# A channel-by-channel FFT convolution stage: the column part of a shift read from memory instead of multiplied by a matrix

## The chip, the cores and the metric

One core of one Trainium2 chip runs the whole program in one launch. The metric is device time in microseconds (us) of that core; the time of a kernel is the median of several executions. A profile is one more execution, recorded by the hardware: instructions of TensorE (PE; its weight loads are PEld), VectorE (DVE), ScalarE (ACT), GpSimd (POOL), the DMA issues of SyncE (SP), and the packets of 16 DMA engines.

## The reference

Four layers with residuals on x of 32 images x 192 channels x 56 x 56, float32. Each layer normalizes its input over 32 groups of 6 channels.

```python
x = x + _L0_conv_ref(_gn(x), ...)   # agent attention, depthwise 3x3 convolution, projection
x = x + _L1_conv_ref(_gn(x), ...)   # bidirectional recurrent scan over the 3136 positions
x = x + _L2_conv_ref(_gn(x), L2_conv_offset)
x = x + _L3_conv_ref(_gn(x), ...)   # 55x55 depthwise convolution with a computed filter, plus bias * x
```

The change is about layer 2. 48 offsets of two numbers each serve four channels apiece. An offset is rounded to a whole shift R in y and x, with zeros where the source lies outside the image; what is left of it, delta, sets a 3x3 Gaussian kernel, which is the product of three row factors and three column factors:

```python
out = shift_one(x, R)                       # zeros from outside
sq = (f[None, None, :] + delta[:, 0]) ** 2 + (f[None, :, None] + delta[:, 1]) ** 2
kern = exp(-sq / (2 * 0.5 ** 2)); kern = kern / kern.sum(axis=(1, 2))
out_LO = conv3x3_depthwise(out, kern, padding=1)
```

Since a layer works on a normalized input, (x - m) / sqrt(var + eps), the kernel keeps the mean m and the factor 1/sqrt(var + eps) beside x and applies them where they fit.

## The kernel before

The program has four stages one after the other: `make_filter` computes the filter of layer 3 and its spectra; `attention` does layer 0 image by image; `scan_pairs` does layer 1 on pairs of images; `channel_blocks` does layers 2 and 3 channel by channel. The first two overlap at their seam and end at about 5180 us, the scan runs to 8360, the channel stage from there to the end. `scan_guarded` is a slower scan that is entered only for extreme values.

**x2.** The scan hands its result to the channel stage through x2 in device memory, laid out as [channel][image parity s][row h, 57 of them][16 image pairs g][56 columns]. The 57th row holds the mean that the normalization needs. One channel is 114 partitions (s, h) x 896 (g, w) floats; a partition's 896 floats lie together, 3584 bytes. rs2 holds the factor 1/sqrt(var + eps) of each channel and image.

**Steps of the channel stage.** The 192 channels form 32 groups of 6, the groups of layer 3's normalization. The loop at the end of `channel_blocks` runs n over 33 values and j over 6; one (n, j) is called a step here. In a step, channel j of group n-1 is analysed (`analyse`), channel j-1 is finished (`synthesise`, the generator `ending`), and group n is prepared: two channels are shifted in each step with j below 3 (`shift`), two are centred in each with j of 3 to 5 (`centre`). The parts are generators, and a written-out order takes turns between them, so that TensorE has matmuls of one part while another waits for its evictions. A scheduler keeps each engine's order close to this; instructions of an engine run in order.

**Shift before.** For one channel `shift` loads x (L1582, on SP's queue), and multiplies from both sides by matrices: eight matmuls (L1589) with the row matrix, which also moves rows and subtracts the mean, then eight (L1607) with the column matrix. VectorE evicts the first with the factor 1/sqrt (L1596), adds the second product to x (L1615, two instructions of 114x448) and sums rows for the next normalization (L1616). The two matrices are made once in four channels by GpSimd (`matrices`, L1542, L1546, L1547), and the row matrix passes once through TensorE (L1550, L1552).

**Centre, analyse, synthesise.** `centre` subtracts the group's mean on VectorE (L1633), squares on ScalarE (L1635) and sums on VectorE (L1636); L1641 and L1642 make layer 3's factor rs from the means (L1624). `analyse` turns rows to spectra with eight matmuls (L1757 in `_rows_to_spectra`; ScalarE copies them out at L1763), columns with six (L1655), and multiplies by the filter's spectrum on VectorE (L1662 to L1668, eighteen instructions). `synthesise` goes back with 32 matmuls (L1681), whose results ScalarE copies out as four z pieces of 84x448 (L1688), and four more (L1698); VectorE multiplies the result by rs (L1700) and adds it to x (L1701), and SP stores x in two halves (L1704).

**Buffers.** x has 15 buffers, the ring `ps` in PSUM four, most work tiles two. x's buffer comes free with the store.

**Start.** The shifts, the Gaussian factors and the validity masks are computed at the beginning of `channel_blocks` by some thirty small operations on 114 partitions.

**SP's queue.** All the loads and stores named here are issued by SyncE, in order. In `attention` it loads the next image while one is worked on, and stores x1 at an image's end. In a step of the channel stage it issues two output stores, the load of a channel and, once a group, factors and spectra.

Of the kernel before, what the change touches and what calls it, by code (L numbers as in the profile page):

```python
# [20 lines left out]
F32 = mybir.dt.float32  # L21
# [7 lines left out]
C = 192  # L29
T = 96  # L30
# [37 lines left out]

def _resize_matrix():

    at = (np.arange(S) + 0.5) * POOL / S - 0.5
    w = np.maximum(0.0, 1.0 - np.abs(at[:, None] - np.arange(POOL)[None, :]))
    return w / w.sum(1, keepdims=True)
# [4 lines left out]
    (114, (2 * 2 * NF,)), (128, (2, 2 * NF)), (84, (2, 2 * S)), (84, (2, 114)), (114, (114,)), (114, (114,)),  # L78
    (114, (114,)), (112, (112,)), (114, (2,)),
# [3 lines left out]
def _constants():  # L83
# [16 lines left out]
    for t in range(2):  # L100
# [17 lines left out]
        "chan_k": _filled([f[n] for n in "f1 f2 f3 f4 ones_rows lags diff_y diff_x at_rows".split()]),  # L118
# [3 lines left out]
def _spectral_constants():  # L122
# [21 lines left out]
    for s in range(2):  # L144
# [7 lines left out]
    col = np.arange(2 * S) % S  # L152
    together = np.arange(2 * S)[:, None] // S == np.arange(2 * S)[None, :] // S
    diff_x = np.where(together, col[None, :] - col[:, None], 1e6)
    at_rows = np.stack([np.concatenate([col, [0, 0]]), row], 1)
# [5 lines left out]
        "ones_rows": ones,  # L161
        "lags": lags,
        "diff_y": diff_y,
        "diff_x": diff_x,
        "at_rows": at_rows,
# [41 lines left out]

@with_exitstack
def make_filter(ctx: ExitStack, tc: tile.TileContext, a, consts, filt, spectra, beside):
# [29 lines left out]
    beside()  # L239
    nd = cp.tile([T, 2], F32, name="nd", tag="nd")  # L240
# [124 lines left out]
def attention(ctx: ExitStack, tc: tile.TileContext, a, ready, x1, st_a, st_c):  # L365
# [48 lines left out]
    for t in (*agents_b[0], *agents_b[1], v_a, v_c):  # L414
        nc.gpsimd.memset(t, 0.0)

# [342 lines left out]
    for b in range(NB):  # L759
# [57 lines left out]
        for h, r in HALVES:  # L817
            nc.sync.dma_start(out=x1[b, 128:C, 1568 * h : 1568 * h + 1568], in_=x[1][r].rearrange("p y x -> p (y x)"))
# [32 lines left out]
def scan_pairs(ctx: ExitStack, tc: tile.TileContext, a, k, x1, st_a, st_c, x2, rs2, count):  # L851
# [86 lines left out]
    kept_a, kept_c = small("kept_a", [128, 2, NB // 4, 2]), small("kept_c", [128, 2, NB // 4])  # L938
# [261 lines left out]
    def conclude(s):  # L1200
# [3 lines left out]
        nc.vector.tensor_copy(kept_a[:, p % 2, p // 2, :], rs[:, 0:2, 0])  # L1204
        nc.vector.tensor_copy(kept_c[:, p % 2, p // 2 : p // 2 + 1], rs[:, 2])
# [46 lines left out]
    for i, r in enumerate((slice(0, 64), slice(64, 128))):  # L1252
        nc.sync.dma_start(out=rs2[128:C, :, :, i], in_=kept_c[r])
# [17 lines left out]
def scan_guarded(ctx: ExitStack, tc: tile.TileContext, a, k, x1, x2, rs2):  # L1271
# [45 lines left out]
    kept = cp.tile([T, 2, 2, NB // 4, 2], F32, name="kept", tag="kept")  # L1317
# [47 lines left out]
    for b in range(NB):  # L1365
# [84 lines left out]
        g, i = b // 4, b // 2 % 2  # L1450
        nc.vector.tensor_copy(kept[:, :, i, g, b % 2], rs)
# [11 lines left out]
def channel_blocks(ctx: ExitStack, tc: tile.TileContext, a, k, x2, rs2, spectra, out):  # L1463
# [11 lines left out]
    PR = 2 * (S + 1)  # L1475
# [6 lines left out]

    NP = C // 4
    off = cp.tile([PR, NP, 2], F32, name="off", tag="off")
    nc.sync.dma_start(out=off, in_=a["L2_conv_offset"].partition_broadcast(PR))
# [8 lines left out]
    f1, f2, f3, f4, ones, lags, diff_y, diff_x, at = pieces  # L1494
# [6 lines left out]
    nc.vector.tensor_scalar(off, off, -(2.0**21), 2.0**21, ALU.max, ALU.min)  # L1501
    rnd = cp.tile([PR, NP, 2], F32, name="rnd", tag="rnd")
    nc.vector.tensor_scalar(rnd, off, BIG, None, ALU.add)
    nc.vector.tensor_scalar(rnd, rnd, BIG, None, ALU.subtract)
    gs = cp.tile([PR, NP * 2, 3], F32, name="gs", tag="gs")
    nc.vector.tensor_tensor(off, off, rnd, ALU.subtract)
    flat = off.rearrange("p n d -> p (n d)")
    for f in range(3):
        nc.vector.tensor_scalar(gs[:, :, f], flat, float(f - 1), None, ALU.add)
    nc.vector.tensor_tensor(gs, gs, gs, ALU.mult)  # L1510
    nc.scalar.activation(gs, gs, AF.Exp, scale=-2.0)
# [384 lines left out]
```

## Time and profile before

| | us |
|---|---|
| median of 3 runs | 12302.43 (12298.38 to 12305.09) |
| profiled execution, time | 12294.66 |
| profiled execution, span | 12292.8 |

Busy time in us by stage, from windows of the trace:

| stage | length | PE | DVE | ACT | POOL | granted PE clock | DMA share |
|---|---|---|---|---|---|---|---|
| filter and attention, 110 to 5180 | 5070 | 4793.9 | 4349.8 | 2771.6 | 177.4 | 0.97 | 0.16 |
| scan, 5180 to 8360 | 3180 | 2644.7 | 3063.2 | 2026.6 | 1753.0 | 0.93 | 0.41 |
| start of channel stage, 8360 to 8420 | 60 | 24.9 | 30.1 | 2.3 | 34.8 | 0.73 | 0.36 |
| channel stage, 8420 to 12150 | 3730 | 3681.9 | 3235.0 | 1330.5 | 283.4 | 1.00 | 0.17 |
| its last steps, 12150 to 12293 | 143 | 134.9 | 104.9 | 52.0 | 0.0 | 0.99 | 0.14 |

The DMA share is the mean busy share of all 16 engines: a transfer that runs on six of them alone shows at most 0.38. A float32 matmul leaves two records, and records of successive matmuls and VectorE operations overlap a little, so a mean duration is longer than the distance from one instruction to the next.

### The profile page before, as it was taken

The numbers are of one execution on the slowest core, as the hardware profiler recorded it, in microseconds if no ns is written. First come the engines' busy times: TensorE is split into PE (matmuls) and PEld (weight loads), VectorE is DVE, ScalarE is ACT, GpSimd is POOL, SyncE is SP. The second block draws the span as 40 slices with busy tenths as digits, with TensorE's granted clock in tenths as the row PEclk, the third lists the DMA queues.
The fourth block names the chain that finished last, engine by engine and source line by source line (L and its number), as shares of the span: only waits on it lengthen the run. The fifth ranks groups of instructions, "written<-read, shape, count | busy, mean of one in ns | idle before, by whom it ended". The sixth has DMA issues, their size and how long they took to land. (4 is left out here: it accounts for less than half of the span.)

```text
span 12292.8 us, 164375 instructions
## 1 busy us (share of the span) xinstructions
PE 11329.2 (92%) x62734; PEld 7107.7 (58%) x62734; DVE 10836.4 (88%) x15489; ACT 6205.0 (50%) x11808; POOL 2250.7 (18%) x2228
## 2 busy tenths in 40 slices
PE   7999999999999999788888888888999999999999
PEld 3555555655555555333333333336777777777777
DVE  6888888888888887999999999997888888888888
ACT  3555555555555554566666666663333333333333
POOL 0000000000000000655555555551000000000000
PEclk9999999999999999999999999999999999999999
DMA  2111111111111111244344433442111111111111
GB/s 69 40 42 46 52 41 40 40 40 40 40 40 40 42 50 44 75 103 100 95 97 103 101 94 97 103 101 65 44 41 45 41 44 42 44 42 44 42 43 29
DMA packets 930055, 719.69 MB, mean 59 GB/s; under 512 B 770325, under 2 KB 807236, under 8 KB 920124
## 3 DMA queue, kind: packets, MB, share of 16 engines
q1 hardware_dynamic: 919020, 683.39, 21.7%
q10 hardware_dynamic: 10240, 25.70, 0.8%
q8 instruction: 500, 8.19, 0.3%
q14 instruction: 295, 2.42, 0.1%
HBM read 403.47 MB, written 240.65 MB: 52 GB/s over the span
## 5 line engine op out<-in xcount | busy, mean ns | idle before, releaser
L572 DVE SCALAR_TENSOR_TENSOR o<-v_a,att_w,o 128x896 f32<-128x896 f32 (+1 forms) x1024 | 1053.8, 1029 | 418.6 <-ACT v_a L546 291.5
L1763 ACT COPY y<-ps 64x252 f32<-64x252 f32 (+1 forms) x2376 | 808.2, 340 | 1135.0 <-PE ps L1757 1104.8
L1681 PE MATMUL ps<-fixed,real 84*84 84x112 f32 x6144 | 1090.9, 259 | 0.0
L1681 PE MATMUL ps<-fixed,imag 84*84 84x112 f32 x6144 | 1089.5, 259 | 0.0
L1688 ACT COPY z<-ps 84x448 f32<-84x448 f32 x768 | 405.6, 528 | 1218.5 <-PE ps L1681 1217.0
L1086 POOL MEMSET f<- 128x1 f32 x96 | 8.9, 99 | 4726.3 <-DMA st_c<-st 4721.3
L1681 PEld LDWEIGHTS ps<-fixed,real 84*84 84x84 f32 x6144 | 784.0, 153 | 134.2 <-issue 95.8
L1681 PEld LDWEIGHTS ps<-fixed,imag 84*84 84x84 f32 x6144 | 763.8, 153 | 0.0
L1079 ACT ACTIVATE q<-q 128x784 f32<-128x784 f32 x384 | 328.2, 855 | 802.5 <-DVE q L1074 633.1
L834 PE MATMUL ps<-sq,fixed 128*128 128x392 f32 x512 | 297.3, 743 | 428.6 <-ACT sq L1157 428.6
L572 DVE SCALAR_TENSOR_TENSOR o<-v_c,att_w,o 128x448 f32<-128x448 f32 (+1 forms) x1024 | 635.0, 620 | 5.1
L585 PE MATMUL ps<-xs_a,gk_a 128*98 128x448 f32 (+1 forms) x1536 | 637.1, 495 | 0.0
L589 ACT ACTIVATE pr<-ps,low 98x896 f32<-98x896 f32 (+1 forms) x384 | 352.3, 918 | 559.9 <-DVE low L587 559.9
L586 PE MATMUL ps<-xs_c,gk_c 125*98 125x448 f32 (+1 forms) x1536 | 631.6, 492 | 0.0
L1547 POOL TENSOR_TENSOR mat<-tap,tap 114x114 f32<-114x114 f32 x96 | 40.8, 425 | 3166.1 <-PE ps L1607 2313.2
L677 PE MATMUL ps<-gq_a,xs_a 128*112 128x294 f32 x1792 | 602.8, 417 | 19.2 <-DVE pq L682 19.2
L1698 PE MATMUL ps<-z,fixed 84*114 84x448 f32 x1536 | 608.8, 539 | 0.0
L834 PE MATMUL ps<-x,weights 128*128 128x392 f32 x1536 | 577.4, 519 | 27.5 <-DVE bv L1108 14.2
L678 PE MATMUL ps<-gq_c,xs_c 125*112 125x294 f32 x1792 | 594.5, 412 | 0.0
L1655 PE MATMUL re<-y,fixed 128*84 128x420 f32 (+1 forms) x1152 | 532.3, 543 | 8.7 <-ACT y L1763 7.6
L1655 PE MATMUL im<-y,fixed 128*84 128x420 f32 (+1 forms) x1152 | 526.9, 538 | 0.0
L690 ACT ACTIVATE pq<-pq 112x1176 f32<-112x1176 f32 x224 | 265.3, 1184 | 498.9 <-DVE pq L682 376.0
(367 smaller groups left out, 29245.2 us busy)
## 6 DMA issues: line engine op xcount, KB each, us to landing
x<-x SPq DMA_DIRECT2D x576, 392.0 KB
x<-x SPq DMA_DIRECT2D x512, 196.0 KB
x<-x SPq DMA_DIRECT2D x192, 399.0 KB
out_x<-x SPq DMA_DIRECT2D x384, 196.0 KB
x<-in_x SPq DMA_DIRECT2D x32, 1568.0 KB
x<-x SPq DMA_DIRECT2D x32, 1568.0 KB
x<-in_x SPq DMA_DIRECT2D x64, 392.0 KB
rd<-rd ACTq DMA_DIRECT2D x128, 196.0 KB
```

What stands on the lines that cost most here:

```text
L572: nc.vector.scalar_tensor_tensor(dst, tap(i), dww[:, t, i : i + 1], dst, ALU.mult, ALU.add)
L585: mm(ps[P2, h, :n], g[:, cols], xs_a[j][:, px], start=True, stop=False)
L586: mm(ps[P2, h, :n], gk_c[0:KC, 2 * j + h, cols], xs_c[j][0:KC, px], start=False, stop=True)
L589: nc.scalar.activation(pr[:, :, :n], ps[P2, :, :n], AF.Exp, bias=low[:, j, p : p + 1], accum_out=sums[:, j, p : p + 1])
L677: mm(ps[:SUB, i, :HA], xs_a[j][:, px], g, start=True, stop=False)
L678: mm(ps[:SUB, i, :HA], xs_c[j][0:KC, px], gq_c[0:KC, 2 * j + (q + i) // ns], start=False, stop=True)
L834: mm(out, aa, srcs[t][h], start=True, stop=False)
L1655: nc.tensor.matmul(ps[:, : n * 84], f2[:, i, :], y[:, i0 : i0 + n].rearrange("p g s u -> p (g s u)"), start=True, stop=True)
L1681: nc.tensor.matmul(ps[:84, i * 2 * S : (i + 1) * 2 * S], part[:, i0 + i].rearrange("p s u -> p (s u)"), f3[:, m, :], start=(m == 0), stop= ...
L1688: nc.scalar.copy(z[:, i0 : i0 + n].rearrange("p g m w -> p (g m w)"), ps[:84, : n * 2 * S])
L1698: nc.tensor.matmul(got, f4[:, m, :], z[:, i0 : i0 + n, m, :], start=(m == 0), stop=(m == 1))
L1763: nc.scalar.copy(y[64 * m : 64 * m + 64, 2 * g0 + i : 2 * (g0 + n) : 2], got[64 * i : 64 * i + 64, :, :, m, :])
```

## The change

Layer 2's column part is no longer a matrix product.

- **x2 is padded in memory.** Each row of 56 columns is followed by 56 zeros (a pitch of 112 floats), with 64 zeros before the first and after the last. A load that begins some columns early or late then reads the shifted row with zeros where the source is outside. Rows of x and of the shifted x are pieces of 224 bytes.
- **The zeros** (`gaps`) are written in `attention`: six channels' gaps at the end of each image, behind its stores of x1 on SP's queue.
- **`_find_shifts`**, new, computes shifts and factors in `make_filter`; the factors (`found`, nine numbers a position) and the first element of each load (`begins`, whole numbers) go to device memory and are loaded at the start of the channel stage. The second mask disappears.
- **`prepare(c)`**, new, is called four channels ahead: it loads the shifted x of channel c with a start read from `begins` (SP reads one register every four channels), into one of three buffers with a zero column at each end. ScalarE multiplies it by the three column factors (one write into `smooth`, two into `more`), and GpSimd adds the products (two additions of 114x896). `spare` is a ring of three buffers for `more`, `moved` and `sq`.
- **`shift`** then needs two matmuls with the row matrix (448 columns each). VectorE evicts them with the factor 1/sqrt into `moved` (two instructions), adds it to x in one (114x896), and sums. x itself is loaded here as before.
- **`matrix`** makes only the row matrix.
- **rs on the spectra's partitions.** `spread` computes layer 3's factor on 84 partitions (matrix `ones_u`). ScalarE's evictions of z multiply by it, image pair by image pair: 16 instructions of 84x112 in place of four of 84x448. L1700 goes, and VectorE adds the last product to x straight from PSUM.
- The written-out order has two turns fewer; `prepare` is called once a step, after it.

In the scan, only the layout of what is kept for rs2 changes.

```diff
+def _find_shifts(nc, cp, a, k, taps, begins):
...
+    nc.vector.tensor_copy(found[:, :, 0:3], gs[:, 0::2])
+    nc.vector.tensor_tensor(found[:, :, 3:6], gs[:, 1::2], _bc(ok, [PR, NP, 3]), ALU.mult)
+    for f in range(3):
+        nc.vector.tensor_scalar(found[:, :, 6 + f], rnd[:, :, 1], float(1 - f), None, ALU.add)
+    nc.sync.dma_start(out=taps, in_=found)
+    first = cp.tile([1, NP], I32, name="first", tag="first")
+    nc.vector.tensor_scalar(first, rnd[0:1, :, 0], -1.0, float(LEAD), ALU.mult, ALU.add)
+    nc.sync.dma_start(out=begins, in_=first)
...
 def make_filter(...):
     beside()
+    _find_shifts(nc, cp, a, consts, *shifts)
...
 def attention(...):
+            stored = nc.sync.dma_start(
+                out=x1[b, 128:C, 1568 * h : 1568 * h + 1568], in_=x[1][r].rearrange("p y x -> p (y x)")
+            )
+        for c in range(C * b // NB, C * (b + 1) // NB):
+            laid = nc.sync.dma_start(
+                out=gaps[c].rearrange("s h g w -> (s h) g w"),
+                in_=zeros[:, 0:S].unsqueeze(1).to_broadcast([2 * (S + 1), NB // 2, S]),
+            )
+            behind = mybir.DependencyInfo(mybir.DependencyClass.NoSync, mybir.DependencyReason.DATA)
+            tc.add_manual_dep(laid.ins, stored.ins.name, behind, reason="no burst")
...
 def channel_blocks(...):
+    shifted = [cp.tile([PR, NI, S + 2], F32, name=f"shifted{i}", tag=f"shifted{i}") for i in range(3)]
+    for t in shifted:
+        nc.gpsimd.memset(t[:, :, 0 : S + 2 : S + 1], 0.0)
...
+    def prepare(c):
...
+        t = shifted[c % len(shifted)]
+        there = flat_x2[bass.ds(begin_at[i] + c * SPAN, SPAN)].rearrange("(p g w) -> p g w", p=PR, w=PITCH)
+        nc.sync.dma_start(out=t[:, :, 1 : S + 1], in_=there[:, :, 0:S])
+        y = wp.tile([PR, NI, S], F32, name="smooth", tag="smooth", bufs=5)
+        taps = [found[:, i, f : f + 1] for f in range(3)]
+        nc.scalar.activation(y, t[:, :, 0:S], AF.Copy, scale=taps[0])
+        for f in (1, 2):
+            more = wp.tile([PR, NI, S], F32, name="more", tag="spare", bufs=3)
+            nc.scalar.activation(more, t[:, :, f : f + S], AF.Copy, scale=taps[f])
+            nc.gpsimd.tensor_tensor(y, y, more, ALU.add)
+        smooth[c] = y
+        rows_of[c] = matrix(i)
...
     def shift(q, j):
-        for g0 in range(0, NG, 4):
-            n = min(4, NG - g0)
+        o = wp.tile([PR, NI, S], F32, name="moved", tag="spare", bufs=3)
+        for g0 in range(0, NI, 8):
+            n = min(8, NI - g0)
+            px = slice(g0 * S, (g0 + n) * S)
             ps = psum()
-            for g in range(n):
-                nc.tensor.matmul(
-                    ps[: 2 * S, g * PR : (g + 1) * PR],
-                    flat[:, (g0 + g) * 2 * S : (g0 + g + 1) * 2 * S],
-                    rows,
-                    start=True,
-                    stop=True,
-                )
+            nc.tensor.matmul(ps[:PR, : n * S], rows, y[:, px], start=True, stop=True)
             nc.vector.tensor_tensor(
+                o[:, g0 : g0 + n],
+                ps[:PR, : n * S].rearrange("p (g w) -> p g w", w=S),
+                _bc(q.scale[:, j, g0 : g0 + n], [PR, n, S]),
                 ALU.mult,
             )
-        yield
-        for g0 in range(0, NG, 4):
...
-            xc = flat[:, g0 * 2 * S : (g0 + n) * 2 * S]
-            nc.vector.tensor_tensor(xc, xc, ps[:PR, : n * 2 * S], ALU.add)
+        nc.vector.tensor_tensor(x, x, o, ALU.add)
         nc.vector.tensor_reduce(q.sums[:, 0, j, :], x, AX.X, ALU.add)
...
     def spread(q):
-        q.rs = sp.tile([PR, NI], F32, name="rs", tag="rs")
-        nc.scalar.activation(q.rs, means(q, 1), AF.Ln, bias=eps)
+        q.rs = sp.tile([84, NI], F32, name="rs", tag="rs")
+        nc.scalar.activation(q.rs, means(q, 1, ones_u), AF.Ln, bias=eps[:84])
...
     def synthesise(q, j, product):
-            nc.scalar.copy(
-                z[:, i0 : i0 + n].rearrange("p g m w -> p (g m w)"), ps[:84, : n * 2 * S]
-            )
+            for i in range(n):
+                nc.scalar.activation(
+                    z[:, i0 + i].rearrange("p m w -> p (m w)"), ps[:84, i * 2 * S : (i + 1) * 2 * S], AF.Copy,
+                    scale=q.rs[:, i0 + i : i0 + i + 1],
+                )
...
-            o = wp.tile([PR, 8, S], F32, name="o", tag="o")[:, :n]
-            nc.vector.tensor_tensor(o, got, _bc(q.rs[:, i0 : i0 + n], [PR, n, S]), ALU.mult)
-            nc.vector.tensor_tensor(x[:, i0 : i0 + n], x[:, i0 : i0 + n], o, ALU.add)
+            nc.vector.tensor_tensor(x[:, i0 : i0 + n], x[:, i0 : i0 + n], got, ALU.add)
...
+    for c in range(4):
+        prepare(c)
...
-                taking, two[0], two[0], taking, ending, ending, two[0], taking, ending, ending, two[1], two[1], taking,
+                taking, two[0], taking, ending, ending, two[0], taking, ending, ending, two[1], taking,
                 ending, two[1], ending,
             ):
                 next(step, None)
+            prepare(n * GROUP + j + 4)
...
+    n = C * 2 * (S + 1) * (NB // 2) * PITCH
+    x1, flat = scratch("x1", [NB, C, N]), scratch("x2", [n + 2 * LEAD])
+    wide = flat[LEAD : LEAD + n].rearrange("(c s h g w) -> c s h g w", c=C, s=2, h=S + 1, w=PITCH)
+    x2, gaps = wide[..., 0:S], wide[..., S:PITCH]
```

## The prediction

> **What bounds the kernel now.** I read the page's busy shares first, then its forty slices, then the busy time of each engine in single steps of the channel stage, then the groups of that stage, and last the DMA view.
>
> The page's busy line and the channel stage step by step (columns: stretch, its length, busy time of PE, weight loads, DVE, ACT, POOL with counts, granted clock, DMA share, GB/s):
>
> ```profile
> PE 11329.2 (92%) x62734; PEld 7107.7 (58%) x62734; DVE 10836.4 (88%) x15489; ACT 6205.0 (50%) x11808; POOL 2250.7 (18%) x2228
> ```
>
> ```profile
> 9031.70:9053.80 22.10, 21.92 (x166) 17.95 (x165) 18.67 (x32) 5.17 (x14) 2.51 (x4) 1.00 0.15 38
> 9053.80:9077.00 23.20, 22.89 (x166) 18.17 (x165) 18.98 (x32) 6.14 (x17) 3.53 (x5) 1.00 0.15 36
> 9100.20:9118.90 18.70, 18.49 (x115) 13.24 (x115) 17.24 (x29) 9.09 (x21) 0.00 (x0) 1.00 0.18 44
> 9118.90:9136.50 17.60, 17.28 (x112) 12.77 (x111) 15.86 (x27) 9.29 (x24) 0.00 (x0) 1.00 0.19 47
> 8600.00:12293.00 3693.00, 3642.40 (x24832) 2805.03 (x24830) 3183.53 (x5354) 1320.17 (x3175) 263.46 (x395) 1.00 0.17 42
> ```
>
> The first two are steps in which two channels are shifted, the next two steps in which two are centred. From one output store to the next, shift steps take about 22.8 us and centre steps 17.3, a group of six 121.1. PE is 98.6% busy over the stage and fills both kinds; DVE is at 84% in shift steps and 91% in centre steps; ACT and POOL have room. So PE sets the pace, and DVE stands 1.5 to 4 us behind it: what PE gains beyond that is cut off by DVE.
>
> The groups of that stage (count, then busy us and mean ns of one; means overlap by 0.07 to 0.1 us on DVE, so I use spacings from the timeline: 0.54 for a 0.612 row, 1.0 for 1.080):
>
> ```profile
> L1589 PE MATMUL ps<-mat,x 114*112 114x114 f32 x2800 | 308.1, 263 | 7.6 <-ACT y L1763 7.6
> L1607 PE MATMUL ps<-mat,turned 112*114 112x112 f32 x2800 | 333.9, 265 | 3.5
> L1698 PE MATMUL ps<-z,fixed 84*114 84x448 f32 x1480 | 586.6, 539 | 0.0
> ```
>
> ```profile
> L1701 DVE TENSOR_TENSOR x<-x,o 114x448 f32<-114x448 f32 x370 | 229.9, 623 | 3.6
> L1700 DVE TENSOR_TENSOR o<-ps,rs 114x448 f32<-114x448 f32 x370 | 225.9, 612 | 5.9 <-PE ps L1698 5.9
> L1633 DVE TENSOR_TENSOR padded<-x,mean 114x896 f32<-114x896 f32 x180 | 194.4, 1080 | 1.0
> ```
>
> ```profile
> L1763 ACT COPY y<-ps 64x252 f32<-64x252 f32 x1464 | 532.1, 363 | 1017.8 <-PE ps L1757 1000.6
> L1688 ACT COPY z<-ps 84x448 f32<-84x448 f32 x739 | 390.3, 528 | 1166.6 <-PE ps L1681 1165.2
> L1635 ACT ACTIVATE sq<-padded 114x896 f32<-114x896 f32 x180 | 171.2, 951 | 66.3 <-DVE padded L1633 63.3
> L1641 ACT ACTIVATE rs<-ps,eps 114x16 f32<-114x16 f32 x30 | 8.2, 274 | 101.5 <-PE ps L1624 101.5
> ```
>
> **The change, part by part: TensorE.** L1589 and L1607 cost 16 records each per channel; on the timeline they issue about 0.11 us apart, 3.5 us a channel. In their place come two matmuls of 448 columns, four records like those of L1698, which issue 0.39 apart: 1.56 us. So 1.94 us less per channel, 3.9 per shift step: 22.8 becomes 18.9 if PE stays gapless. The other bound is the centre step: 17.3 us without any shift work, plus 3.1, is 20.4. Centre steps lose nothing on PE. Half of the matrix work (L1550 stays) goes.
>
> **VectorE.** Per shifted channel two L1615 go (1.1 us) and one 114x896 addition comes (1.0, as L1633); per synthesised channel two L1700 go (1.1). DVE falls from about 18.9 to 17.6 us in shift steps, from about 16.6 to 15.5 in centre steps.
>
> **ScalarE.** Three taps a channel at L1635's 0.951, 2.85 us; and 16 evictions of 84x112 in place of four of 84x448 (2.1 us). An 84x112 one is not in the trace: between 0.22 to 0.27 (114x16 in L1641's pair of rows) and 0.363 (252 columns); I take 0.25, so 4.0. ACT goes to some 11 us in shift steps and 14 in centre steps (15.7 at the dearest). What hides that is a step of 17 to 20 us. It adds a wait, though: the first tap waits for the shifted load, the third's buffer for GpSimd and DVE (a ring of three shared by taps, moved and sq), and behind each in ACT's order stand y copies and z evictions, for which L1655 and L1698 on PE wait.
>
> **GpSimd.** Two 114x896 additions per channel, not in the trace. Low bound 0.95 (the 114x1024 memset's 952 ns); high bound 0.425 x 896/114 = 3.3 (the 114x114 addition, all of it proportional). The memsets of 128 and 1024 columns (205 and 952 ns) give 0.83 ns a column for one access; 782 more columns at one to three of these, on top of 0.428, give 1.1 to 2.4. I take 2.0, so 4.0 us a step, within any step. But DVE pays: at 9030.9 an L1701 lasted 0.77 where its mean is 0.62, while L1547 ran on POOL, and at 9072.9 a tap of POOL took 1.25 instead of 0.76 beside L1664; L1615, which reads PSUM, stayed at 0.61 beside POOL. So operations of DVE with both inputs in SBUF (six of L1664 and L1668, two L1633 or two new additions a step) hold up and are held up. From nothing to the whole 2.0 for each addition; I take half, 1.0, or 2.0 us a step, since DVE has single-source work first in about half of the cases. DVE is then at 19.6 and 17.5.
>
> [...] With every addition blocking DVE for its whole 2.0 us the steps would be 21.6 and 19.5, and nearly nothing would be gained; no row here shows so long an addition.
>
> **DMA.** Rows of x2 are now 224 B apart, so a load of a channel is 1824 packets of 224 B and not 114 of 3584, and there are two. Nine loads in a row of 399 KB at 8390.8 moved 152 GB/s with share 0.33 to 0.38, that is on six of 16 engines. The price of a small packet is seen in the output stores:
>
> ```profile
> DMA packets 1821, 0.42 MB, mean 73 GB/s; under 512 B 1820, under 2 KB 1820, under 8 KB 1820
> q1 hardware_dynamic: 1820, 0.40, 35.1%
> ```
>
> In a stretch of 5.7 us, 35.1% of 16 engines over 1820 packets is 17.6 ns each. By bytes alone, 174 ns for 3584 B, it would be 11; stretches with mixed traffic of 220-byte reads gave up to 30. At 18, a load has 304 packets on each of six engines, 5.5 us; a step has two, a store of 128 packets an engine (2.3) and some 0.5 for the rest: 13.8 us of 19. The cover is the lead of four channels; without it, a step is as long as its loads.
>
> SP: each store (L1704, about 4.2 us before the x load at L1582 follows) now has two loads behind it; the shifted one lands some 17 us after the previous store, inside a step by 2 us.
>
> **Start, attention, head.** Finding shifts moves into the filter part, where DVE stood 17.3 us for its input from 47 to 64 us: -5 to -15, I take -10. Six zero DMAs per image go on SP's queue behind the stores of x1; each is 1824 packets on six engines, 5.5 us, 33 per image in a period of 146.7. The next image's loads and those of gq_c stand behind them. Before, loads issued near 3137 served a DVE operation at 3162; the new order of instructions uses them about 24 us later, and I have them landing some 7 us in time. So zero; without that cover up to 20 us and more an image. At the channel stage's start six channels come as 12 short-packet loads, 66 us, where nine long ones took 26: +35 (to +80).
>
> **The sum.** I take shift steps at 20.2 (between PE's 18.9 and 20.4, DVE's 19.6 with little slack) and centre steps at 17.8 (DVE 17.5). A group: 3 x 38.0 = 114.0 against 121.1, 7.1 less; over 31.5 groups -224. With -10 and +35: -199 from the profiled run's 12294.66 (span 12292.8, 1.9 around it) gives 12,096; that run is 7.8 under the median of 12302.43, so 12,100 for the median. 0.2% of this, 25 us, is what a measurement can tell from no change.
>
> **The rivals.** (A) Slower: the six engines become the bound. From 608 packets at p plus 2.8 = 19.0, it decides from p = 26.6 ns. At 30 ns a step is 21.1, a group 126.4: +5.3 x 31.5 + 65 = about 12,530. For: mixed stretches of 25 to 30. Against: 17.6 in the store.
> (B) DVE and GpSimd: at 3.3 us an addition, blocking 2.3 each, steps are 22.2 and 20.1, a group 127: about 12,510. For: the 0.425 row by proportion. Against: the memset's slope. At 1.7 us of blocking for each, the time is that of before.
> (C) Zeros late: 15 us x 31 images = +465 - 199, 12,570; breaks even at 6.4 us an image. For: the queue is in order. Against: DMA share there is 0.1 to 0.2, and the 7 us.
> (D) No blocking: steps 19.0 and 17.1, a group 108.3: -403 + 25, about 11,920. For: DVE's spare time in shift steps.
> The change not doing what it says (the dynamic load fetching whole rows late) is inside A.
>
> **How the numbers follow.** Forecast (group 111 to 118, 11,990 to 12,230) 0.42; D 0.16; A 0.14; B 0.13; C 0.10; within 25 us of before 0.05. Faster: forecast and D, 0.58; same 0.06 with the edges; slower 0.36. The range drops D's lower part and the worst of A to C: 11,900 to 12,540.
>
> **What would show it.** Right: output stores 20 and 18 us apart, PE near 96%, the new POOL addition near 2 us, DVE two-source rows longer than before by some 0.2, loads landing in 6 us. Wrong: first taps waiting for DMA (A), POOL additions over 3 us or L1664 near 1 us (B), DVE or PE in the attention waiting for x or gq_c and a period over 147 (C).

## The result and the profile after

The changed kernel is slower: 12504.31 us median (12495.53 to 12518.73), 1.0165 times the kernel before (95% interval 1.0148 to 1.0183). The forecast was 12,100. The profiled run has a span of 12504.6, 211.8 longer than before. Four moments of the two traces say where, each read from SP's queue:

| stretch | before | after | difference |
|---|---|---|---|
| start to the scan's first load of statistics | 4886.8 | 4961.6 | +74.8 |
| scan, to the first store of rs2 | 3473.3 | 3469.7 | -3.6 |
| from there to the first output store | 110.8 | 144.9 | +34.1 |
| first output store to the end | 3821.9 | 3928.5 | +106.6 |

Within the first row the first image ends at 344.2 instead of 342.8 (+1.4), an image then takes 147.6 us instead of 146.3 (31 periods, +40.2), and the last image's end is followed by 41.5 us instead of 8.3 until the scan's first load (+33.2). In the last row a group of six takes 124.9 instead of 121.2 (121.1 in the forecast); shift steps 22.6 instead of 23.0, centre steps 19.0 instead of 17.4, all from the distances of output stores, averaged over some 30 groups each.

The page's busy line after, and the steps of one group with the whole stage (columns as before: stretch, length, busy PE, weight loads, DVE, ACT, POOL, granted clock, DMA share, GB/s):

```profile
PE 11189.2 (89%) x57358; PEld 6723.2 (54%) x57358; DVE 10904.3 (87%) x14914; ACT 7160.1 (57%) x14690; POOL 3092.5 (25%) x2376
```

```profile
10021.25:10044.81 23.56, 21.80 (x125) 15.51 (x125) 19.28 (x28) 15.83 (x43) 4.90 (x2) 0.99 0.28 61
10044.81:10067.48 22.67, 20.91 (x110) 13.60 (x108) 19.34 (x28) 11.29 (x32) 4.90 (x2) 0.93 0.26 54
10088.52:10108.45 19.93, 19.93 (x111) 14.76 (x110) 15.90 (x27) 10.49 (x29) 4.48 (x3) 0.83 0.28 60
...
8700.00:12300.00 3600.00, 3325.86 (x18704) 2340.26 (x18702) 3092.05 (x4554) 2101.62 (x5580) 963.13 (x541) 0.94 0.28 60
```

TensorE was busy 98.6% of the stage at clock 1.00; now it is busy 92% at 0.94. No engine is full: the stage waits. The groups of the same stretch show for what (count, then busy us, mean ns, idle before and its releaser):

```profile
L1625 POOL TENSOR_TENSOR smooth<-smooth,more 114x896 f32<-114x896 f32 x346 | 822.3, 2377 | 2622.2 <-ACT more L1624 2609.2
L1723 ACT ACTIVATE z<-ps,rs 84x112 f32<-84x112 f32 x2760 | 741.7, 349 | 555.3 <-PE ps L1715 550.4
...
L1648 DVE TENSOR_TENSOR x<-x,moved 114x896 f32<-114x896 f32 x171 | 346.7, 2028 | 5.9
...
L1702 DVE TENSOR_TENSOR imag<-a,a 84x420 f32<-84x420 f32 x345 | 250.9, 727 | 4.0
L1667 DVE TENSOR_TENSOR padded<-x,mean 114x896 f32<-114x896 f32 x174 | 230.7, 1339 | 1.0
...
L1735 DVE TENSOR_TENSOR x<-x,ps 114x448 f32<-114x448 f32 x345 | 206.9, 607 | 0.0
...
L1621 ACT ACTIVATE smooth<-shifted,found 114x896 f32<-114x896 f32 x171 | 178.4, 1043 | 201.4 <-DMA shifted<-x 171.9 <-PE ps L1641 27.7
```

GpSimd's addition takes 2.38 us. VectorE's addition of 114x896 takes 2.03 where the like row L1633 took 1.08; imag 0.727 where it took 0.585 before; padded 1.34 instead of 1.08. All three have both sources in SBUF. L1735, with one source in PSUM, stays at 0.607. The row of imag before:

```profile
L1668 DVE TENSOR_TENSOR imag<-a,a 84x420 f32<-84x420 f32 x367 | 214.7, 585 | 1.6
```

How this stops TensorE is seen in one shift step, in the timeline (start, duration, engine; in brackets the idle time before and its releaser):

```profile
10036.15 4.98 POOL L1625 TENSOR_TENSOR smooth<-smooth,more 114x896 f32<-114x896 f32 x2 [21.68 <-ACT more L1624]
10036.23 2.95 DVE L1648 TENSOR_TENSOR x<-x,moved 114x896 f32<-114x896 f32 x1
...
10043.05 0.60 DVE L1735 TENSOR_TENSOR x<-x,ps 114x448 f32<-114x448 f32 x1
...
10043.71 0.84 PE L1793 MATMUL ps<-fixed,padded 114*128 114x168 f32 x4 [1.76 <-DVE x L1735]
```

```profile
10044.38 3.12 PE L1641 MATMUL ps<-smooth,rows 114*114 114x448 f32 x4
...
10067.06 1.67 PE L1641 MATMUL ps<-smooth,rows 114*114 114x448 f32 x4
```

POOL starts 0.08 us before L1648, which then lasts 2.95 instead of 1.08. VectorE runs its next operations without a gap, 1.9 us late, up to L1735, which empties a buffer of the ring `ps`; L1793 needs that buffer, and TensorE stands 1.76 us. The next step has the same stop, up to 10066.38. From 8700 to 12000 TensorE waits for VectorE longest, and then for ScalarE's copies of y, while ScalarE's first taps wait for their loads (us in all, times, longest):

```profile
PE ps L1793 <- DVE x L1735: 196.7, 93, 3.6
PE re L1689 <- ACT y L1799: 53.1, 31, 3.9
ACT smooth L1621 <- DMA shifted<-x: 160.9, 40, 7.2
```

After the first stop the four matmul records of L1641 take 3.12 us, after the second 1.67. The granted clock is the reason. The trace's 440 records of it begin at whole multiples of 3.413 us from one another (to 0.02 us). In windows of this length:

```profile
10041.05:10044.46 3.41, 1.65 (x12) 1.40 (x11) 3.41 (x7) 2.91 (x8) 0.08 (x1) 1.00 0.25 55
10044.46:10047.87 3.41, 3.41 (x6) 1.32 (x5) 1.27 (x3) 1.50 (x5) 0.00 (x0) 0.50 0.55 110
...
10061.53:10064.94 3.41, 3.09 (x16) 2.16 (x14) 3.41 (x6) 1.10 (x4) 2.27 (x1) 1.00 0.46 103
10064.94:10068.35 3.41, 1.97 (x8) 1.36 (x9) 2.78 (x6) 2.87 (x9) 0.00 (x0) 1.00 0.07 15
10068.35:10071.77 3.42, 3.42 (x24) 2.41 (x23) 3.33 (x5) 1.22 (x3) 0.00 (x0) 1.00 0.60 121
```

The first stop lies inside one window, which is left 48% busy, and the next window runs at 0.50. The second, equally long, lies across a border; the two windows are 91% and 58% busy, and the clock stays at 1.00. From 8700 to 12300, 82 windows at full clock were idle for half or more of their length, and 81 of them were followed by one at half clock; of the 75 that were idle for 10 to 50%, 17 were, so the profile's idle time is not the whole rule. A stop of 1.8 us can thus cost another 1.7 us of work at half clock. At the mean of 0.94 over 3600 us that is up to 216 us of full-speed work lost in the stage, where the kernel before lost none.

### The profile page after: what moved, and what is told of

The parts are those of the page before. It is cut to its first block, busy times and chain, and to the rows that moved or that the text cites. A ratio compares the mean times of both kernels' runs of the same rounds, so it can differ in the third digit from the quotient of the medians.

```text
span 12504.6 us, 157329 instructions
## 1 busy us (share of the span) xinstructions
PE 11189.2 (89%) x57358; PEld 6723.2 (54%) x57358; DVE 10904.3 (87%) x14914; ACT 7160.1 (57%) x14690; POOL 3092.5 (25%) x2376
## 5 line engine op out<-in xcount | busy, mean ns | idle before, releaser
L1625 POOL TENSOR_TENSOR smooth<-smooth,more 114x896 f32<-114x896 f32 x384 | 908.7, 2367 | 2758.5 <-ACT more L1624 2744.1
L1723 ACT ACTIVATE z<-ps,rs 84x112 f32<-84x112 f32 x3072 | 824.9, 349 | 619.5 <-PE ps L1715 614.5
L1715 PE MATMUL ps<-fixed,real 84*84 84x112 f32 x6144 | 1118.9, 264 | 0.0
L1715 PE MATMUL ps<-fixed,imag 84*84 84x112 f32 x6144 | 1115.5, 264 | 0.0
L1715 PEld LDWEIGHTS ps<-fixed,real 84*84 84x84 f32 x6144 | 815.7, 158 | 165.6 <-issue 130.6
L1715 PEld LDWEIGHTS ps<-fixed,imag 84*84 84x84 f32 x6144 | 790.6, 157 | 11.3 <-issue 11.3
L1793 PE MATMUL ps<-fixed,padded 114*128 114x168 f32 x3072 | 548.4, 328 | 231.4 <-DVE x L1735 224.4
L1793 PEld LDWEIGHTS ps<-fixed,padded 114*128 114x128 f32 x3072 | 485.8, 202 | 308.9 <-DVE x L1735 255.4
L1689 PE MATMUL re<-y,fixed 128*84 128x420 f32 (+1 forms) x1152 | 574.9, 582 | 58.1 <-ACT y L1799 57.9
```

What stands on the lines that cost most here:

```text
L1625: nc.gpsimd.tensor_tensor(y, y, more, ALU.add)
L1689: nc.tensor.matmul(ps[:, : n * 84], f2[:, i, :], y[:, i0 : i0 + n].rearrange("p g s u -> p (g s u)"), start=True, stop=True)
L1715: nc.tensor.matmul(ps[:84, i * 2 * S : (i + 1) * 2 * S], part[:, i0 + i].rearrange("p s u -> p (s u)"), f3[:, m, :], start=(m == 0), stop= ...
L1723: nc.scalar.activation(z[:, i0 + i].rearrange("p m w -> p (m w)"), ps[:84, i * 2 * S : (i + 1) * 2 * S], AF.Copy, scale=q.rs[:, i0 + i : i ...
L1793: nc.tensor.matmul(ps[:, g * 168 : (g + 1) * 168], flat[:, (g0 + g) * 128 : (g0 + g + 1) * 128], f1, start=True, stop=True)
```

## The experiments

A ratio is to the kernel before on the same chip; "group" is the mean distance over six output stores. Before has 121.2, the change 124.9.

### GpSimd's additions away, or on VectorE

```diff
-            nc.gpsimd.tensor_tensor(y, y, more, ALU.add)
```

> The changed kernel with GpSimd's two additions per channel left out (smooth holds the first tap alone, the two other taps are still computed on ScalarE; the shifted part of the output is incomplete). Theory L (each addition holds off VectorE's two-source operations, VectorE's backlog stops TensorE, and TensorE's clock falls after the stop): the addition of moved returns from 2.03 to about 1.1 us, the granted clock of the channel stage from 0.94 to at least 0.98, shift steps from 22.6 to about 19.5, a group from 124.9 to 111 to 115, the time to 12,060 to 12,200. Rival D (the short-packet loads or ScalarE's longer queue set the step): a group stays above 121, the time above 12,380.

12190.97 us, ratio 0.9917 (0.9900 to 0.9933), group 114.3. The two-source rows are back at 1.092, 0.586 and 1.081, the clock at 0.98:

```profile
9000.00:11900.00 2900.00, 2807.64 (x16463) 1971.87 (x16462) 2470.93 (x4013) 1844.88 (x4906) 140.38 (x175) 0.98 0.31 67
```

Some ten of the 124.9 us hang on these additions, though GpSimd itself was idle three quarters of the time. Group and time lie where theory L had them; first taps still wait 165 us for their load.

```diff
-            more = wp.tile([PR, NI, S], F32, name="more", tag="spare", bufs=3)
-            nc.scalar.activation(more, t[:, :, f : f + S], AF.Copy, scale=taps[f])
-            nc.gpsimd.tensor_tensor(y, y, more, ALU.add)
+            nc.vector.scalar_tensor_tensor(y, t[:, :, f : f + S], taps[f], y, ALU.mult, ALU.add)
```

> The changed kernel with the second and third tap as one multiply-add each on VectorE (114x896, about 1.05 us each), in place of ScalarE's product and GpSimd's addition: VectorE gets 2.1 us more work a channel, GpSimd's additions go. Theory L: VectorE's two-source rows return to those of before (0.585, 1.08), the clock to 0.98 or more, a group to 114 to 119, the time to 12,160 to 12,320. Rival D, or VectorE simply full: a group of 122 to 128, the time 12,400 to 12,600.

12347.58 us, ratio 1.0046 (1.0029 to 1.0063), group 119.1. Rows and clock (0.99) came back as expected; the two operations take 1.147 each. Group and time lie just above theory L's ranges and below the rival's. 2.3 us of VectorE's own work a channel cost less than holding it off; ScalarE also loses two taps here, which this run does not part from it. VectorE is 91% busy, but it is not shown to be the bound: TensorE's longest wait, in a stretch of 3200, ends with ScalarE's copies.

```profile
PE ps L1791 <- ACT y L1797: 185.8, 197, 2.5
```

### Long loads

```diff
-        there = flat_x2[bass.ds(begin_at[i] + c * SPAN, SPAN)].rearrange("(p g w) -> p g w", p=PR, w=PITCH)
-        nc.sync.dma_start(out=t[:, :, 1 : S + 1], in_=there[:, :, 0:S])
+        there = flat_x2[bass.ds(begin_at[i] + c * SPAN, SPAN // 2)].rearrange("(p w) -> p w", p=PR)
+        nc.sync.dma_start(out=t.rearrange("p g w -> p (g w)")[:, 0 : NI * S], in_=there)
...
-        nc.sync.dma_start(out=x, in_=x2[c].rearrange("s h g w -> (s h) g w"))
+        there = flat_x2[LEAD + c * SPAN : LEAD + c * SPAN + SPAN // 2].rearrange("(p g w) -> p g w", p=PR, w=S)
+        nc.sync.dma_start(out=x, in_=there)
```

> The changed kernel with both loads of a channel reading 3584 bytes in a row per partition, not 224 at a time (same bytes, wrong places; layer 2 and 3 get other data). Rival D: first taps no longer wait for the load (172 us in all now), a group falls below 119, the time below 12,330. Theory L: a group stays within 2 us of 124.9; the start of the channel stage is 25 to 40 us shorter; the time is 12,420 to 12,480.

12516.21 us, ratio 1.0184 (1.0167 to 1.0201), group 125.1: no gain, as theory L has it, but the start only 6 us shorter, not 25 to 40, and the time above both ranges. First taps waited more, not less (384 us in a stretch of 3200, against 161 in 3300).

> GpSimd's additions left out as in e1_no_add, and both loads long as in e3_long (layer 2 and 3 get other data). In e1 a group still takes 114.3 us and ScalarE's first taps wait 165 us for their load. If late loads are what is left there: a group falls to 108 to 112, the time by 70 to 200 to 11,990 to 12,120. If ScalarE's in-order queue and TensorE set it: a group of 113.5 to 115, the time within 40 us of e1's ratio.

12324.14 us, ratio 1.0025 (1.0015 to 1.0035), group 119.6: five microseconds longer than with short loads. Neither expectation. In the timeline of ScalarE the first tap now stands right behind its load, 5.9 us after its issue at 10012.07, where in e1 one stood 13.3 us after (10009.51 to 10022.82). Over the stage the median distance is 6.3 us here and 8.4 in e1. That the scheduler takes the long load to be faster, and so draws the tap closer, is the likely reason. The load and its tap in this run:

```profile
10012.07 0.99 SPq L1618 DMA_DIRECT2D shifted<-x  x1
```

```profile
10017.92 1.04 ACT L1621 ACTIVATE smooth<-shifted,found 114x896 f32<-114x896 f32 x1 [6.21 <-DMA shifted<-x]
```

So these two runs changed the order as well as the loads, and they clear the packets' size only so far: shorter transfers do not help where the tap is drawn closer to them.

### The sum of x from PSUM

```diff
-        o = wp.tile([PR, NI, S], F32, name="moved", tag="spare", bufs=3)
...
-            nc.vector.tensor_tensor(
-                o[:, g0 : g0 + n],
-                ps[:PR, : n * S].rearrange("p (g w) -> p g w", w=S),
-                _bc(q.scale[:, j, g0 : g0 + n], [PR, n, S]),
-                ALU.mult,
-            )
-        nc.vector.tensor_tensor(x, x, o, ALU.add)
+            got = ps[:PR, : n * S].rearrange("p (g w) -> p g w", w=S)
+            nc.vector.tensor_tensor(got, got, _bc(q.scale[:, j, g0 : g0 + n], [PR, n, S]), ALU.mult)
+            nc.vector.tensor_tensor(x[:, g0 : g0 + n], x[:, g0 : g0 + n], got, ALU.add)
```

> The changed kernel, GpSimd's additions kept, with the scaled product written back to PSUM in place and added to x from there (two additions of 114x448 with one source in PSUM, in place of one of 114x896 with both in SBUF). Theory L in its narrow form (only an operation with both sources in SBUF is held off): the new additions take 0.61 each, GpSimd's addition stays near 2.1 to 2.4, TensorE's stops in shift steps go, a group falls from 124.9 to 115 to 119.5, the time to 12,200 to 12,340. Rival (GpSimd slows whatever VectorE does beside it): the new additions last 0.8 or more, a group stays above 122.

12266.28 us, ratio 0.9979 (0.9969 to 0.9988), group 117.0. The additions last 0.613 beside the same GpSimd work; what is left of the holds moved to the products, which still have both sources in SBUF:

```profile
L1625 POOL TENSOR_TENSOR smooth<-smooth,more 114x896 f32<-114x896 f32 x336 | 758.5, 2261 | 1832.2 <-ACT more L1624 1470.5 <-ACT smooth L1621 349.1
L1697 DVE TENSOR_TENSOR imag<-a,a 84x420 f32<-84x420 f32 x336 | 298.4, 888 | 3.9
...
L1643 DVE TENSOR_TENSOR x<-x,ps 114x448 f32<-114x448 f32 x338 | 207.1, 613 | 5.9
```

The narrow form of L holds in these rows: where a source lies, not how much is added, decides (0.613 for 114x448 with one source in PSUM; 0.888 for 84x420 with both in SBUF, where L1668 took 0.585 before). `moved` also leaves the ring `spare` here, but that ring had stopped nobody: the second and third taps (L1624) of the change had 0.0 us of idle time before them.

### ScalarE's evictions, and the load's place

```diff
-            for i in range(n):
-                nc.scalar.activation(
-                    z[:, i0 + i].rearrange("p m w -> p (m w)"), ps[:84, i * 2 * S : (i + 1) * 2 * S], AF.Copy,
-                    scale=q.rs[:, i0 + i : i0 + i + 1],
-                )
+            nc.scalar.copy(z[:, i0 : i0 + n].rearrange("p g m w -> p (g m w)"), ps[:84, : n * 2 * S])
...
+            o = wp.tile([PR, 8, S], F32, name="o", tag="o")[:, :n]
+            nc.vector.tensor_tensor(o, got, _bc(q.rs[:, i0 : i0 + n], [PR, n, S]), ALU.mult)
-            nc.vector.tensor_tensor(x[:, i0 : i0 + n], x[:, i0 : i0 + n], got, ALU.add)
+            nc.vector.tensor_tensor(x[:, i0 : i0 + n], x[:, i0 : i0 + n], o, ALU.add)
```

> The changed kernel with ScalarE's four plain evictions of z and VectorE's product with rs put back (layer 3's factor on 114 partitions as before). ScalarE gets some 3.4 us less a step, VectorE 1.1 more. If ScalarE's 16 small evictions cost part of the time: a group falls below 122. Theory L, with VectorE as the engine that is short: a group of 126 to 130, the time 12,540 to 12,670.

12309.92 us, ratio 1.0014 (1.0004 to 1.0023), group 117.9, against theory L's 126 to 130: with 1.1 us more on VectorE the group is 7 us shorter, while x<-x,moved is still held (1.746). First taps wait 23 us for their loads, where they waited 161. So ScalarE's queue is a second cause.

> The changes of e6_psum and e7_copies together, GpSimd's additions kept. Each alone took a group from 124.9 to 117.0 and 117.9. If the two causes (VectorE held off; ScalarE's queue of small evictions) are separate stops of TensorE: a group of 112 to 115.5, the time 12,130 to 12,220. If they are one stop seen from two sides, or VectorE is full (it gets 1.1 us a step back): 116 to 118, the time 12,230 to 12,300.

12318.05 us, ratio 1.0020 (1.0011 to 1.0030), group 118.5, just above the second expectation: the cures do not add. The rows show what happens: L1700's old pair brings an operation with both sources in SBUF back, and it and the products take the holds that L1648 took:

```profile
L1728 DVE TENSOR_TENSOR x<-x,o 114x448 f32<-114x448 f32 x333 | 294.7, 885 | 1.0
...
L1693 DVE TENSOR_TENSOR real<-a,a 84x504 f32<-84x504 f32 x167 | 204.8, 1226 | 0.0
```

> e1_no_add (GpSimd's two additions left out, the shifted part incomplete) with the plain evictions of e7_copies. With nothing holding VectorE off and ScalarE short of 2 us less, what is left is TensorE's own work: 108 to 112 a group if the prediction's sum for TensorE (18.9 and 17.1 to 17.3 a step) is right; 113.5 or more if VectorE's extra 1.1 us or late loads bind. The time 11,990 to 12,110, or 12,160 and more.

12143.74 us, ratio 0.9878 (0.9861 to 0.9894), group 112.6, between the two expectations; shift steps 20.4, centre steps 17.2. TensorE is 97.8% busy at clock 1.00:

```profile
9000.00:11900.00 2900.00, 2835.06 (x16733) 1989.74 (x16732) 2661.19 (x4385) 1552.44 (x3134) 155.35 (x175) 1.00 0.32 68
```

This is nearly what TensorE's work alone allows: at the upper end of the 18.9 to 20.4 that the forecast gave a shift step.

To tell small evictions from waiting taps, the load alone (register, address and transfer, as `fetch`) moves one step ahead of the taps in `prepare`:

```diff
-    shifted = [cp.tile([PR, NI, S + 2], F32, name=f"shifted{i}", tag=f"shifted{i}") for i in range(3)]
+    shifted = [cp.tile([PR, NI, S + 2], F32, name=f"shifted{i}", tag=f"shifted{i}") for i in range(4)]
...
+            fetch(n * GROUP + j + 5)
             prepare(n * GROUP + j + 4)
```

> The changed kernel with each shifted load issued one step earlier (a fourth buffer), its taps where they were. Theory W (first taps wait in ScalarE's in-order queue for their load: 5.9 us a group): these waits fall below 1 us a group and a group from 124.9 to 119 to 122, the time by 90 to 180. Rival (ScalarE has room for them, TensorE waits for VectorE alone): waits go, a group stays at 124 to 126.

12395.65 us, ratio 1.0105 (1.0062 to 1.0148), group 120.0. The taps' waits fell from 160.9 to 16.0 us in a stretch of 3300, the group by 4.9. TensorE still waits 212 us for VectorE there, but its wait for copies of y fell from 53.1 to 2.1 us:

```profile
PE ps L1805 <- DVE x L1744: 212.2, 109, 2.5
PE re L1698 <- ACT y L1811: 2.1, 14, 0.2
ACT smooth L1630 <- DMA shifted<-x: 16.0, 14, 2.0
```

So the two stops are separate: between 4 and 5 us a group are taps that wait in ScalarE's queue for their load, with y copies and z behind them (by the rows, the holds fell by some 1 us a group at the same time). The other 2 us of e7 belong to the evictions themselves or to the order around them; no run parts these.

### The zeros

```diff
-                out=gaps[c].rearrange("s h g w -> (s h) g w"),
-                in_=zeros[:, 0:S].unsqueeze(1).to_broadcast([2 * (S + 1), NB // 2, S]),
+                out=x2[LEAD + c * span : LEAD + (c + 1) * span].rearrange("(p i w) -> p i w", p=128, i=12),
+                in_=zeros.unsqueeze(1).to_broadcast([128, 12, span // 1536]),
```

> The changed kernel with each channel's region zeroed as one block on 128 partitions (1536 pieces of 532 bytes, the data's places too, which the scan fills later) in place of 1824 pieces of 224 bytes from 114 partitions. Theory Q (the zeros on the queue cost the scan's first load its 33 us and attention its 1.3 us an image): an image's zeros take 10 to 15 us, the scan starts 50 to 65 us earlier, the time is 12,440 to 12,455. Rival O (the order of instructions costs the 1.3 us an image): only some 20 us at the scan's start are won, 12,485, and the image period stays at 147.6.

12530.94 us, ratio 1.0198 (1.0181 to 1.0215): wrong for both. Twice the bytes (798 KB a channel) moved at about 140 GB/s, and the view shows the DMA engines at 90% or more in every slice; SP still took 27 us to issue an image's six; the period rose to 148.6 and the scan still started 39 us after the last image. Pieces of 3192 bytes were not measured: beside the wider tile of zeros that they need, 11.9 KB a partition of SBUF were left for tiles of `attention` that take 14.2 (e4_wide).

In the next, `asks[-1]` is the write of gq_c; the transfers at the image's end go.

```diff
             if j == 0:
                 gq = seen(ag, wqT, gq_c, "gq_a")
+                for c in range(C * b // NB, C * (b + 1) // NB):
+                    laid = nc.sync.dma_start(
+                        out=gaps[c].rearrange("s h g w -> (s h) g w"),
+                        in_=zeros[:, 0:S].unsqueeze(1).to_broadcast([2 * (S + 1), NB // 2, S]),
+                    )
...
+                    tc.add_manual_dep(laid.ins, asks[-1].ins.name, behind, reason="no burst")
```

> The changed kernel with the same six zero transfers an image, but queued on SP behind the write of gq_c in the middle of the image, ahead of nothing for some 90 us, and no longer between an image's stores and the next image's loads. Theory P (their place on the queue costs it all: the order that is laid out around them 1.3 us an image, the last image's zeros 33 us at the scan's start): the image period is back at 146.2 to 146.6, the scan starts 65 to 80 us earlier than with the change, the time is 12,410 to 12,435. Rival (their packets slow attention's other transfers wherever they lie): the period stays above 147.2, the time 12,455 to 12,470.

12422.39 us, ratio 1.0101 (1.0085 to 1.0118). The period is 146.18, the scan starts at 4885.6, 76 us earlier than with the change and as early as before. The same transfers in another place on the queue cost nothing: after the change, SP's queue held the next image's load for 30.8 us, now it is issued 1.9 us after the stores of x1.

```profile
3015.84 1.23 SPq L865 DMA_DIRECT2D x<-x  x2
3017.12 30.83 SPq L869 DMA_DIRECT2D x<-zeros  x6
3048.00 5.77 SPq L392 DMA_DIRECT2D x<-in_x  x1
```

```profile
3136.23 1.23 SPq L874 DMA_DIRECT2D x<-x  x2
3138.11 0.67 SPq L392 DMA_DIRECT2D x<-in_x  x1
```

No engine's wait on a late x appears in attention after the change. So the zeros' place on the queue costs the 1.3 us an image, but how is not shown; an order of VectorE's and TensorE's work that was laid out around the later load is the likely way. The 33 us before the scan are plain queueing.

> e8_both with the zeros of e9_mid. If the parts add: e8's time less 65 to 80 us, 12,060 to 12,150, about 1.5% under the kernel before. If an earlier scan start is given back later: e8's time less under 30.

12245.84 us, ratio 0.9961 (0.9947 to 0.9975): 72 us under e8_both. This part adds.

### All holds but one taken away

```diff
             nc.vector.tensor_tensor(a0, f[0], gr.to_broadcast(shape), ALU.mult)
-            nc.vector.tensor_tensor(a1, f[1], gi.to_broadcast(shape), ALU.mult)
-            nc.vector.tensor_tensor(to[0], a0, a1, ALU.subtract)
...
-            nc.vector.tensor_tensor(a0, f[0], gi.to_broadcast(shape), ALU.mult)
+            nc.vector.tensor_tensor(f[0], f[0], gi.to_broadcast(shape), ALU.mult)
             nc.vector.tensor_tensor(a1, f[1], gr.to_broadcast(shape), ALU.mult)
-            nc.vector.tensor_tensor(to[1], a0, a1, ALU.add)
+            nc.vector.tensor_tensor(f[1], f[1], gi.to_broadcast(shape), ALU.mult)
+            nc.vector.tensor_tensor(to[0], a0, f[1], ALU.subtract)
+            nc.vector.tensor_tensor(to[1], a1, f[0], ALU.add)
```

> e6_psum with four of the six products of each batch formed so that one source of each sum and difference is in PSUM, and the zeros queued as in e9_mid. Only centre's subtraction still has both sources in SBUF. Theory L, narrow form: real and imag rows return to 0.58, a group goes from e6's 117.0 towards e1's 114.3 (113 to 115.5), the time to 12,080 to 12,160. Rival (VectorE's holds were already of no account in e6, or PSUM buffers held longer stop TensorE): a group of 116.5 or more, 12,180 and more.

12122.11 us, ratio 0.9860 (0.9844 to 0.9877), group 113.9, as theory L has it. GpSimd adds as before, now nearly unhindered at 2.09, and none of the rows with one source in PSUM is longer than it was:

```profile
L1627 POOL TENSOR_TENSOR smooth<-smooth,more 114x896 f32<-114x896 f32 x338 | 705.1, 2090 | 1829.5 <-ACT more L1626 1454.9 <-ACT smooth L1623 362.3 <-POOL smooth L1627 0.2
L1645 DVE TENSOR_TENSOR x<-x,ps 114x448 f32<-114x448 f32 x346 | 212.4, 614 | 6.0
L1697 DVE TENSOR_TENSOR real<-a,im 84x420 f32<-84x420 f32 x347 | 201.6, 581 | 0.0
...
L1664 DVE TENSOR_TENSOR padded<-x,mean 114x896 f32<-114x896 f32 x174 | 193.5, 1131 | 1.0
```

This is the fastest kernel of the study that computes everything: 1.4% under the one before, 3% under the change, with the same arithmetic on the same engines. Some 75 us of that are the zeros' place of e9_mid; they do not touch the group.

> e13_psum_all with ScalarE's four plain evictions of z and VectorE's factor rs applied in PSUM in place (as e7_copies, but without a two-source operation in SBUF). Without GpSimd's additions that gave 112.6 a group (e12). Theory L, narrow form: 112.5 to 115, 12,050 to 12,130. If VectorE is full by then: 116 to 118, 12,170 to 12,220.

12176.59 us, ratio 0.9900 (0.9883 to 0.9916), group 115.9, just below the second expectation; the time is inside it. With the holds gone, the change's move of rs to ScalarE is worth 2 us a group. That VectorE is what is short by then is not shown: it is 88% busy, and TensorE's longest wait ends with ScalarE's copies of y (167.5 us in a stretch of 3200).

> e14_psum_copies with the loads of e15_early. With e14's queue short on ScalarE already, theory W expects little: 0 to 2 us a group below e14. More than 3 us would mean that late loads were still a stop in e14; a longer group that the order of instructions got worse.

12168.85 us, ratio 0.9892 (0.9876 to 0.9909), group 115.6: within 0.3 of e14, as theory W has it for a short queue.

## Why the prediction was wrong, step by step

**Where the difference lies.** The profiled run is 211.8 us longer; the sum had it 199 shorter. Of these 411 us the channel stage's steps make 331 (+106.6 for -224), and the way to the scan 85 (+74.8 for -10).

**TensorE's share was there, at its low end.** The sum's bounds were 18.9 to 20.4 a shift step; e12 shows 20.4 with TensorE 97.8% busy. Of the 3.9 us a step that 18.9 stood for, 2.6 came: 23.0 became 20.4.

**The step that failed is the sum's "shift steps at 20.2 ... DVE's 19.6 with little slack", and with it centre steps at 17.8.** They take 22.6 and 19.0. The size of the hold was right: additions put at 2.0 us take 2.09 to 2.38, the 12 us of holds a group that were taken are about 10 in the rows (six L1648 at 0.95 more, twelve pairs of 84x420 products at 0.24 more, six L1667 at 0.26 more), and VectorE's busy time in the shift steps shown is 19.3, close to the 19.6. The use made of it was wrong: it was added to VectorE's busy time and compared with TensorE's, as if a hold cost nothing while the sum stays under the step. In the trace one hold comes at one place, VectorE is late for everything behind it, a PSUM buffer comes late, and TensorE stops (197 us in a stretch of 3300) though VectorE is 82 to 85% busy in that step; and the stop costs again by the clock, 0.94 for 1.00, which the forecast did not have at all. With the holds gone but for one row (e13) a group takes 113.9.

Rival B had the two engines, but the same adding up, with 2.3 us of blocking from a 3.3 us addition; a 2.4 us addition was enough. That its 12,510 is so near is luck: it had a group of 127 and nothing lost in attention, where a group took 124.9 and attention lost 75 us.

**ScalarE was counted by its load alone.** The forecast named the wait of the first tap and what stands behind it, then gave it no price, "a step of 17 to 20 us" being its cover. Here the in-order queue had no such cover: 4 to 5 us a group (e15). ScalarE's own work was priced well: the 84x112 eviction, put at 0.25, has a mean duration of 0.349, but these overlap, and 2760 of them keep ScalarE busy for 741.7 us, 0.27 each.

**DMA: the price was high, the conclusion right.** Loads at the start of the stage move at 104 GB/s, 399 KB in about 3.9 us, not 5.5. Rival A did not come: with the same loads e12 takes 112.6 a group. How many engines carry a load is not shown; the DMA share in these stretches is 0.45 to 0.47, more than the 0.38 of six engines.

**Attention: the 7 us of slack held, and yet "zero" failed.** No load came late, but 75 us went: 33 in the queue ahead of the scan, which the forecast never looked at, 40 in the longer image period and 1.4 by the end of the first image. Rival C had the place, the queue, but not the mechanism, loads that come late, and put 465 us where 75 were lost.

**The start.** +34 against +35 taken is luck: with long loads it is +28, with long loads and no additions +20, with no additions alone +36, so transfers are not most of it. What the rest is stays open. The filter's -10 did not come: the first image ends at 344.2 instead of 342.8.

That e13_psum_all has 113.9 a group, where the sum had 114.0, does not make the sum right: the sum held VectorE off for 2 us a step and counted that as free, and e13 has almost nothing that holds it off.

## What to carry to other kernels

Before giving GpSimd work beside a busy VectorE, list VectorE's operations with both sources in SBUF. Here one of 1.08 us lasted 2.95 beside GpSimd's additions of 2 to 2.4, and writing one operand back to PSUM in place removed the hold for at most one more VectorE instruction a channel. Price a hold by what stands behind it on the critical engine, not by adding it to a busy share; and a transfer that nobody waits for can still cost its time to what is queued behind it: here the zeros of an image held the next image's load for 30.8 us.

## What was not expected of the hardware

A stop of TensorE of 1.76 us was followed by 3.41 us at half clock in one step and by none in the next; what differed was whether it lay inside one 3.413 us window of the clock, left 48% busy, or across two, 91% and 58% busy. Plain blocks of zeros, 532 bytes a piece from 128 partitions, went to memory at about 140 GB/s (e4b_wide) with the DMA engines at 90% or more in every slice, where 224-byte pieces from 114 partitions went at 72 GB/s with a share of about half (the change): an image's zeros, twice the bytes, took some 39 us instead of 36.
